# Four row tiles' neighbour lists, not two, made inside layer 1's loop of a four-layer graph network

## The chip, the cores and the metric

One core of a Trainium2 chip runs the whole kernel. The metric is the device time of one execution in microseconds, the median of three runs. The engines are TensorE (PE in the profile, its weight loads PEld), VectorE (DVE), ScalarE (ACT), GpSimd (POOL) and SyncE (SP), whose queue issues most transfers; ScalarE's queue issues the writes of the transposed matrix. Each engine and each queue works in order.

## The reference: what is computed

There are 2708 nodes with 128 features. The adjacency matrix `adj` (2708 x 2708, f32) is sparse, with values in [0.05, 1): some 16 entries a row, and the diagonal is always there. Each of four layers takes h = relu(layernorm(x)) and adds its result to x:

```python
# layer 0: mean over a node's columns
msg = jnp.matmul(H.T, X); inv_deg = 1.0 / H.sum(axis=0)
return msg * inv_deg[:, None]
# layer 1: a message for each pair (i, j), weighted by adj
s = node_feats @ msg_w[:, :D].T
d = node_feats @ msg_w[:, D:].T
messages = jax.nn.gelu(s[:, None, :] + d[None, :, :] + msg_b, approximate=False)
aggregated = jnp.einsum('ijd,ij->id', messages, adj)
new_feats = jnp.concatenate([node_feats, aggregated], -1) @ upd_w.T + upd_b
h = gelu(new_feats) + node_feats, then a layer norm with ln_w, ln_b
# layer 2: agg = adj @ states, then a GRU cell
# layer 3: graph attention with two heads, masked by adj > 0 or the diagonal
```

Only layer 1 needs to know which entries are not zero: a Gelu for each of 7.3 million pairs would be too much, so the kernel lists the entries.

## The kernel before, in words

**Tiles and lists.** Nodes come in 22 row tiles of 128 (the last has 20). Columns come in 22 blocks of 124. For each row tile n and block b, VectorE's `max` finds the eight largest values of each row and `max_index` their columns: one *list* (lines 357 and 359, in `list_cut`). A block that holds part of the diagonal is listed from a copy `near` with the diagonal blanked; a row tile has two such blocks.

**Layer 0's loop** (lines 541 to 586) goes over six column cuts c of 512 columns, and within each over six row groups s of four row tiles. Cuts 0 to 4 are steps of their own; the sixth (148 columns, tiles `z`) is worked beside the fifth. At each step VectorE lists the step's blocks (four per row tile), SyncE's queue issues the load of a later step into one of `RING` = 4 buffers (`rows_a`), and TensorE transposes the step's blocks and sums h times the matrix (`work_cut`): a *turn* is four transposes and one sum. ScalarE copies each transposed bank out into one of ten buffers (`turned`) and adds up the degrees on the way; the write of that buffer to `adjT` in device memory is issued one turn later. A load buffer is free when TensorE, VectorE and GpSimd have all read it.

Some lists are not made in this loop: for row tiles from `LATER` = 19 on (but the last, tile 21), the blocks away from the diagonal, 20 in each of tiles 19 and 20, are loaded again in layer 1's loop and listed there, `AT_ONCE` = 3 in a period (`load_late`, `list_late`). The last row tile, of 20 rows, is loaded in one piece at period `WIDE_AT` and listed by `list_wide`; `place_wide` moves these lists to their place by DMA.

**Between the layers** (lines 604 to 636 and 1082 to 1094) VectorE lists the sixth cut's blocks of tiles 4 to 21, and the first three row tiles are prepared for layer 1.

**Layer 1's loop** (`period`, line 1003) has one period for each row tile t and six blocks k in a period. In a period TensorE adds sources and destinations for tile t's entries in `combine` (six bf16 products for each block of 128 entries), ScalarE takes the Gelu (`activate`), and `gather` multiplies by the put tiles, which hold the adjacency values at their rows. Meanwhile the next three tiles go through a pipeline, all in program order on each engine:

- for tile t+4, `count_rows` counts the entries of each row and block;
- for tile t+3, `rank` (TensorE) sums the counts, `spread_ends`, `describe_next` and `select_rows` (all on VectorE, with ScalarE and GpSimd) split the f32 values in three bf16 parts and build the row selector `sel`; two DMAs shift it by one row, and `finish_rows` subtracts;
- for tile t+2, `fetch` (TensorE) brings the entries to their slots and `place` (VectorE) picks value and column;
- for tile t+1, `pass_on` sends the columns to all partitions by DMA, `columns` makes the equality tile `cols`; GpSimd (`put_values`) and ScalarE (`put_more`) make the put tiles.

Every second period `sources` prepares the source rows of the next two tiles. `split` cuts a value in three: ScalarE copies the lead part, VectorE subtracts it, ScalarE copies the second part, GpSimd subtracts.

**Updates.** After four row tiles (a group g; the groups are 0 to `LAST` = 5) the aggregate goes through `mix` (TensorE) and eight `update` steps: bias (VectorE), Gelu (ScalarE), residual and statistics (VectorE), factors (VectorE), scaling (ScalarE, then GpSimd), residual and statistics (VectorE), factors (VectorE), scaling to h (ScalarE). A table says at which period and block each step is issued. The last group's steps are issued in layer 2's first chunk (line 1464), between the pieces of `aggregate`, whose products read h and the transposed matrix.

The order of the instructions is the one in which the program issues them; no scheduler moves them.

## Time and profile before

| what | us |
|---|---|
| median of three runs (1030.32, 1031.84, 1036.13) | 1031.84 |
| the profiled execution | 1032.76 |
| its span, first to last instruction | 1031.0 |
| layer 0's loop, start of the span to its last sums | 0 to about 209 |
| between the layers | 209 to 262 |
| layer 1's periods, steady | 262 to 588 |
| layers 2 and 3 | 588 to 1031 |

TensorE is busy 922.2 us of the span, VectorE 797.4, ScalarE 532.7, GpSimd 470.9; the mean granted TensorE clock is 0.946. Of the line groups, 342 lists from load buffers take 78.9 us in `max` and 91.8 us in `max_index`.

How to read it: a row of a timeline is start, duration, engine, line, operation, output and inputs, shape, number of instructions, and in brackets the time that the engine sat idle before it and who released it. A row of the waits is engine, tile and line, then who was waited for: microseconds in total, how many times, the longest. The granted clock is a share of full speed. A matmul in f32 shows as two instructions. Busy times of PE contain the pipeline's overlap, so 26.00 of 26.00 says that there was no gap, not that the array was at its peak.

### The profile page before, as it was taken

The numbers are of one execution on the slowest core, as the hardware profiler recorded it, in microseconds if no ns is written. First come the engines' busy times: TensorE is split into PE (matmuls) and PEld (weight loads), VectorE is DVE, ScalarE is ACT, GpSimd is POOL, SyncE is SP. The second block draws the span as 40 slices with busy tenths as digits, with TensorE's granted clock in tenths as the row PEclk, the third lists the DMA queues.
The fourth block names the chain that finished last, engine by engine and source line by source line (L and its number), as shares of the span: only waits on it lengthen the run. The fifth ranks groups of instructions, "written<-read, shape, count | busy, mean of one in ns | idle before, by whom it ended". The sixth has DMA issues, their size and how long they took to land. (4 is left out here: it accounts for less than half of the span.)

```text
span 1031.0 us, 22163 instructions
## 1 busy us (share of the span) xinstructions
PE 922.2 (89%) x7948; PEld 747.7 (73%) x7948; DVE 797.4 (77%) x2753; ACT 532.7 (52%) x1561; POOL 470.9 (46%) x588
## 2 busy tenths in 40 slices
PE   6699798955899999999998899999888999999983
PEld 3355354624799999999998844444578999989972
DVE  7999798977677788977767366666578977997793
ACT  5755556734666666676675513333322543654342
POOL 6322222422977798897877264334311300340042
PEclk9999899955899999999999999999989999999996
DMA  9799799512333333333131455565311475457000
GB/s 298 260 314 374 248 365 389 209 65 84 102 121 110 119 109 114 124 101 115 66 114 56 156 187 188 187 204 201 111 48 46 143 233 182 135 164 240 5 15 16
DMA packets 83194, 162.90 MB, mean 158 GB/s; under 512 B 14672, under 2 KB 30148, under 8 KB 83074
## 3 DMA queue, kind: packets, MB, share of 16 engines
q1 hardware_dynamic: 63094, 129.25, 38.7%
q10 hardware_dynamic: 19980, 32.14, 8.6%
q8 instruction: 64, 1.05, 0.4%
q14 instruction: 56, 0.46, 0.1%
HBM read 114.74 MB, written 30.87 MB: 141 GB/s over the span
## 5 line engine op out<-in xcount | busy, mean ns | idle before, releaser
L806 POOL TENSOR_SCALAR put<-count,line,value 128x128 f32<-128x128 f32 x176 | 197.6, 1136 | 32.8 <-DVE value L795 32.6
L1187 PE MATMUL att<-hv,wt 128*128 128x129 f32 x1672 | 195.6, 278 | 7.8 <-DVE wt L1157 6.4
L1187 PEld LDWEIGHTS att<-hv,wt 128*128 128x128 f32 x1672 | 191.9, 194 | 10.9 <-DVE wt L1157 8.9
L888 PE MATMUL p_m<-s,sel 128*128 128x128 bf16 x1452 | 163.5, 221 | 8.5 <-ACT g L900 6.1
L892 PE MATMUL p_m<-d,cols 124*128 124x128 bf16 (+1 forms) x1452 | 163.5, 221 | 5.2 <-DVE cols L837 5.2
L1157 DVE SCALAR_TENSOR_TENSOR wt<-row,lift,mask 128x1024 f32<-128x1024 f32 (+1 forms) x132 | 138.8, 1082 | 22.1 <-PE att L1187 22.0
L120 POOL TENSOR_TENSOR n_r<-n_r,minus_half 128x4 f32<-128x4 f32 (+1 forms) x28 | 39.8, 1420 | 232.0 <-DVE n_r L119 226.9
L913 PE MATMUL agg<-put,g 128*128 128x128 f32 (+1 forms) x968 | 124.1, 281 | 0.0
L381 PE MATMUL sums<-a,h 128*128 128x512 f32 x220 | 119.4, 640 | 1.6 <-ACT h L136 1.6
L395 PEld LDWEIGHTS p_T<-ident,a 128*128 128x128 f32 (+1 forms) x440 | 55.4, 146 | 84.8 <-ACT aT L400 39.7
L913 PEld LDWEIGHTS agg<-put,g 128*128 128x128 f32 x968 | 114.7, 194 | 0.0
L888 PEld LDWEIGHTS <-sel 128*128 128x128 bf16 x1452 | 104.8, 98 | 10.6 <-issue 9.9
L1348 PE MATMUL p_agg<-a,hs 128*128 128x512 f32 (+2 forms) x264 | 108.4, 552 | 2.2 <-DMA a<-adjT 2.1
L892 PEld LDWEIGHTS <-cols 124*128 124x128 bf16 (+1 forms) x1452 | 103.8, 98 | 6.3 <-DVE cols L837 6.3
L395 PE MATMUL p_T<-ident,a 128*128 128x128 f32 (+1 forms) x440 | 73.3, 287 | 30.6 <-ACT aT L400 24.0
L815 ACT ACTIVATE put<-mine,value 128x128 f32<-128x128 bf16 x308 | 100.5, 391 | 0.0
L900 ACT ACTIVATE g<-p_m 128x512 f32<-128x512 f32 x132 | 72.7, 551 | 52.0 <-PE agg L913 41.0
L359 DVE FIND_INDEX8 col<-val,a 128x8 uint16<-128x124 f32 x342 | 91.8, 280 | 0.0
L357 DVE MAX8 val<-a 128x8 f32<-128x124 f32 x342 | 78.9, 271 | 7.6 <-DMA a<-in_adj 7.6
L1348 PEld LDWEIGHTS p_agg<-a,hs 128*128 128x128 f32 (+1 forms) x264 | 47.4, 192 | 49.8 <-issue 46.3
L400 ACT ACTIVATE aT<-p_T 128x512 f32<-128x512 f32 (+2 forms) x132 | 70.9, 539 | 23.9 <-PE p_T L395 18.4
L1310 ACT ACTIVATE hs<-hs 128x1354 f32<-128x1354 f32 (+1 forms) x44 | 58.5, 1329 | 39.3 <-DMA hs<-in_adj 38.9
(287 smaller groups left out, 1556.6 us busy)
## 6 DMA issues: line engine op xcount, KB each, us to landing
hs<-in_adj SPq DMA_DIRECT2D x42, 677.0 KB
adjT<-aT ACTq DMA_DIRECT2D x105, 256.0 KB
a<-adjT SPq DMA_DIRECT2D x20, 1280.0 KB
spread<-passed SPq DMA_DIRECT2D x22, 704.0 KB
later<-sel SPq DMA_DIRECT2D x22, 616.0 KB
a<-in_adj SPq DMA_DIRECT2D x5, 1152.0 KB
a<-in_adj SPq DMA_DIRECT2D x5, 1120.0 KB
a<-in_adj SPq DMA_DIRECT2D x5, 1088.0 KB
```

The lines of the kernel that those rows point to most:

```text
L357: nc.vector.max(val[0:m, n, b, :], v)
L359: nc.vector.max_index(col[0:m, n, b, :], val[0:m, n, b, :], v)
L381: nc.tensor.matmul(accs[c][:, 0:w], h0[0:m, n, :], a[0:m, n - g0, t0 * P - lo : t0 * P - lo + w], start=(n == 0), stop=(n == NT - 1),)
L395: nc.tensor.transpose(p[0:k, i * iw + q * P : i * iw + q * P + m], a[0:m, q, e : e + k], ident[0:m, 0:m])
L806: nc.gpsimd.tensor_scalar(st["put", 0][:, b, :], count, st["line"][:, b : b + 1], st["value"][:, b : b + 1], ALU.is_equal, ALU.mult,)
L815: nc.scalar.activation(st["put", 1][:, b - HP, :], st["mine"][:, b - HP, :], AF.Identity, scale=st["value"][:, b : b + 1])
L888: nc.tensor.matmul(p[:, b - b0, :], st["sel"][:, b, :], s3[:, q, t % 2, :], start=(q == 0), stop=False)
L892: nc.tensor.matmul(p[:, b - b0, :], st["cols"][0:kb, b, :], d3[0:kb, b, q, :], start=False, stop=(q == 2))
L913: nc.tensor.matmul(agg, g[:, b - 4 * k, :], put, start=(b == 0), stop=False)
L1157: nc.vector.scalar_tensor_tensor(wt[:, 0:n], row[:, k, c : c + n], lift[:, j, k : k + 1], mask[:, j, c : c + n], op0=ALU.max, op1=ALU.mult,)
L1187: nc.tensor.matmul(banks[s // 3][:, s % 3, :], wt[:, q * P : (q + 1) * P], hv[:, j, k, :], start=(v < 2 and s // 3 not in touched), stop=( ...
L1348: nc.tensor.matmul(pa[:, 0:n], h[0:k, j, :], a[0:k, j - j0, 0:n], start=(j == 0), stop=(j == NT - 1))
```

## The change

- `LATER` is NT - 5 = 17: lists of row tiles 17 to 20 away from the diagonal, 80 instead of 40, are made in layer 1's loop, `AT_ONCE` = 5 in a period: two at k = 1 and three at the period's end. `WIDE_AT` becomes 17 (it was 15).
- Layer 0 has five load buffers, and six write buffers for the transposed tiles.
- In a period, the describing of the next tile is cut in two. ScalarE's lead copy is issued at k = 1, the subtractions after `select_rows` at k = 2. `sources` is cut in the same way.
- The update steps are issued after `place`, `finish_rows` and the late loads of their block, two blocks later than before for most groups. The last two groups of layer 1's loop have tables of their own, and the final two steps of group 4 are issued in layer 2, after the last group's first two.
- `count_rows` of the last two tiles moves to the end of the period before.

```diff
--- before.py
+++ after.py
@@ -186,8 +186,9 @@
     for q in range(2):
         nc.gpsimd.tensor_copy(xb[q][:, :, 4 * S : 4 * S + R], part.unsqueeze(1).to_broadcast([P, NB, R]))
 
-    LATER = NT - 3
-    AT_ONCE = 3
+    LATER = NT - 5
+    AT_ONCE = 5
+    EARLY = 2
     WIDE = 4
 
     def near_blocks(n):
@@ -281,7 +282,7 @@
             scale_rows([dst[:, t + q, 0:D]], [xs[:, t + q, :]], r[:, q : q + 1], b[:, q : q + 1], AF.Relu)
             yield
 
-    RING = 4
+    RING = 5
     WINDOW = CH + 16 * (len(GROUPS) - 2)
     l0, ending = ExitStack(), ExitStack()
     ordered = ExitStack()
@@ -290,7 +291,7 @@
     once0 = l0.enter_context(tc.tile_pool(name="l0h", bufs=1))
     pool = l0.enter_context(tc.tile_pool(name="l0k", bufs=2))
     marked = l0.enter_context(tc.tile_pool(name="l0n", bufs=8))
-    turned = l0.enter_context(tc.tile_pool(name="l0t", bufs=10))
+    turned = l0.enter_context(tc.tile_pool(name="l0t", bufs=6))
     sump = l0.enter_context(tc.tile_pool(name="l0p", bufs=3, space=PSUM))
     turnp = l0.enter_context(tc.tile_pool(name="l0q", bufs=3, space=PSUM))
     h0 = once0.tile([P, NT, D], F32, name="h0")
@@ -611,11 +612,25 @@
         nc.scalar.copy(dst[1], rest)
         nc.gpsimd.tensor_tensor(dst[2], rest, dst[1], ALU.subtract)
 
-    def describe(t, rest):
+    def lead_of(dst, src):
+        nc.scalar.copy(dst[0], src)
+
+    def rest_of(dst, src, rest):
+        nc.vector.tensor_tensor(rest, src, dst[0], ALU.subtract)
+        nc.scalar.copy(dst[1], rest)
+        nc.gpsimd.tensor_tensor(dst[2], rest, dst[1], ALU.subtract)
+
+    def values_of(t):
+        return [xb[t % 2][:, :, q * S : (q + 1) * S] for q in range(3)], val[:, t, :, :]
+
+    def describe_columns(t):
         x = xb[t % 2]
-        split([x[:, :, q * S : (q + 1) * S] for q in range(3)], val[:, t, :, :], rest)
         nc.gpsimd.tensor_copy(x[:, :, 3 * S : 4 * S], col[:, t, :, :])
         nc.gpsimd.tensor_copy(x[:, :, C - 1], ends[:, t, :])
+
+    def describe(t, rest):
+        split(*values_of(t), rest)
+        describe_columns(t)
 
     for n in range(4, 14):
         list_last(n)
@@ -689,15 +704,15 @@
             units = late_blocks[(t - 1) * AT_ONCE : t * AT_ONCE] if t > 0 else []
             if not units:
                 return
-            cols = work.tile([P, WIDE, JB], F32, name="cols_a")
+            cols = work.tile([P, AT_ONCE, JB], F32, name="cols_a")
             state["late", t] = []
             for i, (n, b) in enumerate(units):
                 m, k = size(n), width(b)
                 nc.sync.dma_start(cols[0:m, i, 0:k], adj[n * P : n * P + m, b * JB : b * JB + k])
                 state["late", t].append((n, b, cols[0:m, i, 0:k]))
 
-        def list_late(t):
-            units = state.pop(("late", t), [])
+        def list_late(t, first, last):
+            units = state.get(("late", t), [])[first:last]
             for n, b, a in units:
                 nc.vector.max(val[0 : size(n), n, b, :], a)
             for n, b, a in units:
@@ -707,7 +722,7 @@
         pieces = [(b, min(WIDE, NB - 1 - b)) for b in range(0, NB - 1, WIDE)]
 
         def load_wide():
-            cols = state["wide"] = work.tile([P, WIDE, JB], F32, name="cols_a")
+            cols = state["wide"] = work.tile([P, AT_ONCE, JB], F32, name="cols_a")
             for i, (b, k) in enumerate(pieces):
                 nc.sync.dma_start(
                     cols[i * TAIL : (i + 1) * TAIL, 0:k, :],
@@ -735,6 +750,10 @@
 
         def describe_next(t):
             describe(t, once.tile([P, NB, S], F32, name="v_r"))
+
+        def describe_rest(t):
+            rest_of(*values_of(t), once.tile([P, NB, S], F32, name="v_r"))
+            describe_columns(t)
 
         def select_rows(t):
 
@@ -866,8 +885,14 @@
                     mq = size(2 * k + q)
                     nc.vector.tensor_tensor(sb[0:mq, q, :, :], pv[0:mq, q, :, :], bv[0:mq, :, :], ALU.add)
             s3 = three.tile([P, 3, 2, D], BF16, name="s3")
-            rest = once.tile([P, 2, D], F32, name="s_r")
-            split([s3[:, q, :, :] for q in range(3)], sb[:, :, 0, :], rest)
+            lead_of([s3[:, q, :, :] for q in range(3)], sb[:, :, 0, :])
+            state["sb"] = sb
+            own_rows[k] = s3, None
+
+        def sources_rest(k):
+
+            sb, s3 = state.pop("sb"), own_rows[k][0]
+            rest_of([s3[:, q, :, :] for q in range(3)], sb[:, :, 0, :], once.tile([P, 2, D], F32, name="s_r"))
             gs = three.tile([P, 2, D], F32, name="gs")
             nc.scalar.activation(gs, sb[:, :, 1, :], AF.Gelu)
             for q in range(2):
@@ -981,14 +1006,14 @@
         GB = (NB + 3) // 4
         mixes, updates = {}, {}
         for g, (first, n) in enumerate(GROUPS[:-1]):
-            at, apart = (first + n + 1) * GB + 1, GB
-            if g == LAST - 2:
-                apart = GB // 2
-            elif g == LAST - 1:
-                at, apart = at - GB + 2, 1
-            mixes[divmod(at, GB)] = g
-            for step in range(STEPS):
-                updates.setdefault(divmod(at + 1 + step * apart, GB), []).append((g, step))
+            at = (first + n + 1) * GB
+            mixes[divmod(at + 1 if g < LAST - 1 else at - 3, GB)] = g
+            steps = {
+                LAST - 1: [at - 2, at - 1, at, at + 1, at + 2, at + 5],
+                LAST - 2: [at + 4, at + GB + 4, at + 2 * GB + 4, *(at + 3 * GB + q for q in (0, 1, 2, 4, 5))],
+            }.get(g, [at + 4 + step * GB for step in range(STEPS)])
+            for step, when in enumerate(steps):
+                updates.setdefault(divmod(when, GB), []).append((g, step))
 
         def check_lists():
             over = fix.tile([P, 2], F32, name="over1")
@@ -1035,23 +1060,28 @@
                 if k in (1, 2) and b:
                     fetch(t + 2, k - 1)
                 if k == 1 and a:
-                    describe_next(t + 3)
+                    lead_of(*values_of(t + 3))
+                if k == 1:
+                    list_late(t, 0, EARLY)
+                    if t == WIDE_AT:
+                        list_wide()
                 if k == 2:
                     if now and t % 2 == 0 and t + 2 < NT:
                         sources(t // 2 + 1)
                     if a:
                         select_rows(t + 3)
-                    if now and t + 4 < NT:
+                        describe_rest(t + 3)
+                    if now and t % 2 == 0 and t + 2 < NT:
+                        sources_rest(t // 2 + 1)
+                    if now and t + 4 < NT - 2:
                         count_rows(t + 4)
-                for g, step in updates.pop((t, k), ()):
-                    update(g, step)
                 if k == 1 and t == NT - 2:
                     check_lists()
                 if k > 0 and c:
                     put_more(t + 1, k)
                 if k == 3 and c:
                     columns(t + 1)
-                if k == 3 and t == WIDE_AT + 1:
+                if k == 3 and t == WIDE_AT:
                     place_wide()
                 if k == 3 and b:
                     place(t + 2)
@@ -1061,10 +1091,12 @@
                     load_late(t + 1)
                     if t + 1 == WIDE_AT:
                         load_wide()
+                for g, step in updates.pop((t, k), ()):
+                    update(g, step)
                 if k == GB - 1:
-                    list_late(t)
-                    if t == WIDE_AT:
-                        list_wide()
+                    list_late(t, EARLY, AT_ONCE)
+                    if now and NT - 2 <= t + 4 < NT:
+                        count_rows(t + 4)
 
 
         def fetch_both(t):
@@ -1084,7 +1116,7 @@
             (finish_rows, 0), (fetch_both, 0), (spread_ends, 1), (select_rows, 1), (rows, 4),
             (split_destinations, 3), (turn_rows, 4), (place, 0), (destinations, 4), (pass_on, 0), (list_last, 18),
             (finish_rows, 1), (fetch_both, 1), (split_destinations, 4), (destinations, 5), (spread_ends, 2),
-            (select_rows, 2), (sources, 0), (describe_next, 2), (columns, 0), (place, 1), (split_destinations, 5),
+            (select_rows, 2), (sources, 0), (sources_rest, 0), (describe_next, 2), (columns, 0), (place, 1), (split_destinations, 5),
             *((list_last, n) for n in range(19, NT)),
             (close_lists, 0),
         ):
@@ -1465,11 +1497,14 @@
             pa = accs.tile([P, CH], F32, tag=f"acc{g % 2}", name="p_agg")
             if g == 0:
                 update(LAST, 0)
+                update(LAST, 1)
+                update(LAST - 1, 6)
+                update(LAST - 1, 7)
             for i, j0 in enumerate(range(0, NT, PIECE)):
                 aggregate(t0, k0, pa, j0)
                 if g > 0:
                     continue
-                for step in ((1, 2), (3, 4), (5,), (6, 7), ())[i]:
+                for step in ((2,), (3, 4), (5,), (6, 7), ())[i]:
                     update(LAST, step)
                 if i == 2:
                     nc.gpsimd.memset(mask[:, NT - 1, :], 0)
```

## The prediction

> **What bounds the kernel now.** I read the page's slices first, then busy times by stretch, then the chain of waits on each side of the places the change touches, last the instruction lists there. Three stretches matter: layer 0's loop (up to 209 us), layer 1's loop (262 to 588) and the first sums of layer 2 (588 to 614). Columns: stretch, its length, busy time of TensorE (PE), its weight loads, VectorE (DVE), ScalarE (ACT), GpSimd (POOL), granted clock, DMA share, GB/s.
>
> ```profile
> 26.00:52.00 26.00, 17.77 (x66) 9.10 (x64) 26.00 (x176) 18.30 (x70) 9.21 (x33) 0.93 0.77 261
> 52.00:78.00 26.00, 26.00 (x118) 15.03 (x119) 25.90 (x177) 15.43 (x59) 4.94 (x12) 1.00 0.96 315
> 78.00:104.00 26.00, 24.75 (x118) 14.64 (x117) 25.39 (x171) 15.23 (x56) 6.92 (x24) 1.00 1.03 373
> 104.00:130.00 26.00, 20.43 (x69) 9.94 (x68) 19.02 (x124) 14.89 (x61) 7.25 (x16) 0.84 0.79 251
> 130.00:156.00 26.00, 25.45 (x123) 15.38 (x122) 25.75 (x170) 13.57 (x46) 6.50 (x20) 0.96 1.03 365
> 156.00:182.00 26.00, 21.28 (x108) 13.00 (x107) 21.79 (x148) 15.57 (x58) 4.60 (x11) 1.00 1.05 389
> 182.00:208.00 26.00, 23.64 (x138) 16.36 (x136) 25.86 (x166) 21.51 (x77) 12.61 (x36) 1.00 0.52 194
> 208.00:262.00 54.00, 26.39 (x153) 17.70 (x151) 39.21 (x143) 21.32 (x71) 14.87 (x25) 0.52 0.20 67
> 262.00:588.00 326.00, 315.96 (x4468) 310.16 (x4468) 245.60 (x602) 211.37 (x639) 261.80 (x260) 0.98 0.34 111
> 588.00:614.00 26.00, 23.24 (x54) 10.12 (x54) 14.09 (x40) 4.11 (x12) 16.01 (x16) 0.87 0.37 117
> ```
>
> In layer 0 VectorE has no room in five of the seven stretches, and its two gaps (104 to 130, 156 to 182) are waits for loads. TensorE is close behind, DMA at or above a share of 1 in three. In layer 1 TensorE is the bound (316.0 of 326), VectorE at 75%. What a layer-0 load waits for, how fast lists go, and the load that came late:
>
> ```profile
> SPq L317 <- PE sums L381: 40.7, 13, 6.3
> SPq L317 <- DVE col L359: 39.1, 9, 8.6
> ...
> SPq L323 <- DVE col L359: 12.5, 3, 5.5
> ```
>
> ```profile
> 81.46 0.46 DVE L357 MAX8 val<-a 128x8 f32<-128x124 f32 x2
> ...
> 82.35 0.46 DVE L357 MAX8 val<-a 128x8 f32<-128x124 f32 x2
> ...
> 130.15 0.48 DVE L357 MAX8 val<-a 128x8 f32<-128x124 f32 x2 [6.26 <-DMA a<-in_adj]
> ```
>
> Two lists take 0.89 us, so a list costs **0.446 us**. A load waits for a buffer that VectorE or TensorE still holds. At 130 a buffer was not filled in time: the clock went to half.
>
> In layer 1 and behind it, TensorE's own waits:
>
> ```profile
> 446.01 0.33 PE L888 MATMUL p_m<-s,sel 128*128 128x128 bf16 x3 [1.57 <-ACT g L900]
> 506.62 0.33 PE L888 MATMUL p_m<-s,sel 128*128 128x128 bf16 x3 [1.84 <-ACT g L900]
> 543.51 0.34 PE L892 MATMUL p_m<-d,cols 124*128 124x128 bf16 x3 [2.25 <-DVE cols L837]
> 591.09 0.79 PE L944 MATMUL p_u<-upd_wT,aggT 128*128 128x128 f32 x2 [2.76 <-ACT aggT L927]
> ```
>
> ```profile
> DVE v_r L610 <- ACT xb L609: 36.0, 16, 3.9
> ...
> DVE s_r L610 <- ACT s L609: 12.6, 10, 1.3
> ```
>
> The last fence is VectorE idle 48.6 us of layer 1 in front of the two subtractions, waiting for a ScalarE copy that stands behind other ScalarE work.
>
> **The change, part by part.** The profiled execution took 1032.76 us (span 1031.0, 1.8 around it); the median of the three runs is 1031.84. I sum against 1032.76.
>
> 1. *Lists out of layer 0.* Row tiles 17 and 18 have 22 blocks each, two of them near the diagonal and kept: 40 lists go (423 to 383). Of these 32 stand in the first four column sweeps, 4 in the fifth, 4 after the loop. The loop's 36 are 36 x 0.446 = 16.1 us of VectorE. The 4 late ones (1.8 us) sit beside waits for the shifted rows and I cost them at nothing; at most 0.9 us of them is exposed, before the second tile's shift.
> What is late next? Floors from 26 to 182 (156 us): VectorE is busy 143.9, less 32 x 0.446 = 14.3, so 129.6. TensorE is busy 135.7, less 7.0 lost to half clock (26 x 0.07, 0.16 and 0.04), so 128.7. DMA moved 58.6 MB from 0 to 182 (26 us times each row's GB/s, with 299 for 0 to 26), and at the best row's 389 GB/s needs 151 of those 182. All three would allow more than 16.1, but they now stand within a few per cent of each other and take turns. Bounds: 0 (another bound takes all) and 23.7 (16.1 plus the 7.6 that VectorE waited for loads). I take **-14**: VectorE's busy stretches are what the trace shows as full, and a little is lost to turn-taking.
> A rule speaks against this. The Trainium skill, "DMA: Bandwidth & Descriptors", section Specifications, puts the HBM limit of a core at about 358 GB/s. The trace has a stretch at 389 and one at 373, so it does not hold as a ceiling here; by it DMA would need 164 of 182 us, an estimate, and the gain would still not be cut below 14.
>
> 2. *Five load buffers, six write buffers.* A load is issued one step earlier, which covers the 6.26 above and helps reach the 14. The transposed tiles' buffers fall from ten to six. In the trace's landing events a write lands 2 us after its issue when nothing loads and 6 to 8 us when loads run. A turn of TensorE is 1.30 us (four transposes and a sum). A copy must find the write of six turns before landed: six turns are 7.8 us; copy, one turn of delay and a write of 6.7 us are 0.6 + 1.3 + 6.7 = 8.6. So it could cost 0.8 us in six turns, 18 times in 110 turns: 15 us at worst for 6.7, nothing where latency is only queueing (five writes in flight at 1.30 us each are the 6.7, and fewer in flight land sooner). Bounds 0 and +15; I take 0, because ScalarE never waits for its copy's buffer now and latency and number in flight agree.
>
> 3. *The end of layer 0.* TensorE waits 3.10 us at 212 for the copy that closes VectorE's lists. With VectorE no longer behind, bounds 0 and -3.1: **-2**.
>
> 4. *Lists into layer 1.* 40 x 0.446 = 17.8 us of VectorE, five lists a period in 16 periods where three stood in 14. VectorE goes from 245.6 to 263.4 of 326. Two of the five stand where VectorE waited for ScalarE (the 36.0). ScalarE's lead copy of the next tile's values now runs while VectorE lists and builds the row selector, and the subtraction comes behind. The same for the sources (12.6). Update steps stand behind the placing, no longer ahead of it, so the equality tiles (the 2.25), the row numbers and TensorE's fetch are no longer behind up to 5.4 us of statistics (537.0 to 542.4 in the list). TensorE's idle time is 10.0 us of 326 and half clock costs 0.02 x 326 = 6.5, part of it the start. Bounds: -14 (nearly all of that goes) and +17.8 (all lists on TensorE's path). I take **-6**: the waits named belong to the order that is changed, and VectorE keeps 60 us free.
> ScalarE has a new wait, for the subtraction that now follows the 1.6 us selector. Queued behind it are the second source copy, the Gelu of the own row and put tiles, then g, for which TensorE waits. It gains the slot before. GpSimd's queue keeps its order; its third part of the values comes one block later, for a fetch a period off. On SyncE's queue two more loads of 62 KB a period stand behind the shift of the selector, 0.45 us of issue each: free, at a DMA share of 0.34.
> The page just named (same section) says pieces under 512 B run below line rate; the new loads' rows are 496 B. Its only price here is DMA time in a layer with two thirds of it idle: 0 by both.
>
> 5. *The last list-group's update.* Its final two steps (factors, scaling) move behind the last group's first two. ScalarE's scaling of 1.65 us waited 3.40 for VectorE, and the copy of the aggregate stood behind it: TensorE's 2.76 us at 591. Half clock there costs 26 x 0.13 = 3.4 us. But the last tiles' rows are needed 20 products later (17 us at 0.86), where they now land with about 1 us to spare, so part comes back. Bounds 0 and -6.2; **-4**.
>
> Sum: -14 - 2 - 6 - 4 = -26: 1032.76 - 26 = 1006.8, against the median 1005.8. I say 1006.
>
> **The rivals.**
> - *Layer 0 is bound by TensorE and DMA all along* and gives half. For: TensorE 26.00 of 26.00 from 52 to 78, DMA share over 1 in three rows. Against: both floors are 27 to 31 us below the stretch. -7 there, -1, -4, -3 elsewhere: 1018.
> - *Layer 1 takes it back*: VectorE, late by lists, becomes the bound there. For: VectorE was already busy 14.4 of 15 us in one stretch (413 to 428) and TensorE lost time in it. Against: the waits it is freed of are more than the lists. Gains -16 in layer 0 and -4 after, all 17.8 on the path: 1032.76 - 20 + 17.8 = 1031, no change.
> - *Six write buffers throttle ScalarE* (the other side). For: 8.6 against 7.8 us. With latency L a group of six turns costs L + 1.9 - 7.8 more, 18.3 times. The whole gain of 26 and 5 us more is gone at L = 7.6; at 8.0 it is 38 lost: 1006 + 38 = 1044. So it decides when writes, with one more load in flight, take over 7.6 us in the mean rather than their 6.7. Against: fewer writes in flight land sooner.
> - *The change does not do what it says*: no; the five lists and the order are in the built program, and 383 and 80 lists can be counted.
>
> **How the numbers follow.** About 0.5% (5 us) is what can be told from no change. Forecast case 0.62 (992 to 1013); half gain 0.21 (1013 to 1025); layer 1 takes it back 0.08; write buffers 0.09. Faster: 0.62 + 0.21 = 0.83; same 0.08; slower 0.09. The range is 992 to 1025: low, layer 0 at 23.7 and layer 1 at -10; high, the half-gain rival with some of the write buffers' price.
>
> **What would show it.** Right: layer 0's last sums end near 194 instead of 208; no VectorE wait near 6 us for a load in the loop; layer 1 at 80 lists, VectorE waits before the subtraction of values down from 36 to under 12, TensorE's idle under 6 us in layer 1; no wait at the aggregate's copy. Wrong: ScalarE waiting for write landings in layer 0; a TensorE period over 15.1 us with VectorE named; lists of the last tiles late, so that the ranking product waits for counts at the loop's end.

## The result, and the profile after

The changed kernel takes **1024.76 us** (median of five runs, 1020.77 to 1026.56) against 1031.56 (1030.32 to 1036.13): a ratio of 0.9922, 95% interval 0.9894 to 0.995. It is 0.8% faster, by 7 us and not by the predicted 26. The profiled execution took 1026.56 us, its span is 1024.8.

Four marks cut both spans into the prediction's steps. They are starts of TensorE's products: the last sum of the sixth cut (the 208 of the prediction), the first and the last `combine` product of layer 1, and the first product with `W_msgT` in layer 2.

| stretch, us | before | after | moved | predicted |
|---|---|---|---|---|
| to the sixth cut's last sum | 208.3 | 211.0 | +2.7 | -14 |
| from there to the first `combine` | 39.5 | 39.3 | -0.2 | -2 |
| first to last `combine` | 336.5 | 329.9 | -6.6 | -6 |
| last `combine` to the first `W_msgT` product | 31.6 | 27.6 | -4.0 | -4 |
| the rest | 415.1 | 417.0 | +1.9 | 0 |
| span | 1031.0 | 1024.8 | -6.2 | -26 |

Layer 1 and the step behind it came out as predicted in size. Nearly all of the error (17 of 20 us) lies in layer 0: 40 lists left it and it did not become shorter. Busy times by stretch of the changed kernel (columns as in the prediction):

```profile
52.00:78.00 26.00, 26.00 (x118) 15.00 (x117) 25.90 (x174) 15.62 (x59) 5.43 (x14) 1.00 0.94 318
78.00:104.00 26.00, 24.42 (x87) 12.89 (x86) 21.35 (x144) 13.46 (x50) 6.81 (x24) 0.80 0.94 313
104.00:130.00 26.00, 21.69 (x94) 12.05 (x93) 18.45 (x121) 14.80 (x58) 6.64 (x14) 0.93 0.83 260
...
156.00:182.00 26.00, 22.19 (x93) 12.11 (x92) 11.44 (x77) 17.36 (x68) 5.31 (x13) 0.93 1.04 378
...
262.00:588.00 326.00, 316.82 (x4479) 310.22 (x4479) 263.16 (x732) 214.43 (x653) 256.98 (x263) 0.98 0.38 119
588.00:614.00 26.00, 25.82 (x66) 11.56 (x66) 16.22 (x42) 6.92 (x14) 16.36 (x15) 1.00 0.64 214
```

VectorE, nearly full in layer 0 before, is now idle for more than half of 156 to 182 (11.44 of 26), and TensorE is hardly fuller (22.19, before 21.28). Behind layer 1 TensorE has next to no gap and full clock (25.82 of 26 at 1.00; before 23.24 at 0.87). Where VectorE's time went, in its waits from 26 to 210 us, first before and then after:

```profile
DVE val L357 <- DMA a<-in_adj: 7.6, 3, 6.3
DVE inv_deg L430 <- ACT aT L400: 4.1, 1, 4.1
```

```profile
DVE inv_deg L431 <- ACT aT L401: 26.1, 3, 14.5
DVE val L358 <- DMA a<-in_adj: 2.4, 3, 1.4
```

The wait for late loads is gone, as foreseen. In its place VectorE stands 26.1 us in `invert`, which needs the degree sums that ScalarE makes while it copies the transposed tiles out. VectorE now runs ahead of everybody and waits for the same ScalarE that TensorE waits for. That last part could be read before. These are TensorE's gaps of 1 us and more from 26 us to the end of layer 0's loop in the kernel *before*:

```profile
28.16 0.66 PE L395 MATMUL p_T<-ident,a 128*128 128x128 f32 x4 [1.78 <-ACT aT L400]
35.33 0.66 PE L395 MATMUL p_T<-ident,a 128*128 128x128 f32 x4 [1.77 <-ACT aT L400]
...
46.07 0.66 PE L395 MATMUL p_T<-ident,a 128*128 128x128 f32 x4 [2.67 <-ACT aT L400]
82.00 0.66 PE L395 MATMUL p_T<-ident,a 128*128 128x128 f32 x4 [1.25 <-ACT aT L400]
109.81 0.66 PE L395 MATMUL p_T<-ident,a 128*128 128x128 f32 x4 [1.20 <-ACT aT L400]
120.47 0.92 PE L395 MATMUL p_T<-ident,a 128*128 128x128 f32 x4 [3.82 <-ACT aT L400]
...
158.88 0.66 PE L395 MATMUL p_T<-ident,a 128*128 128x128 f32 x4 [1.78 <-ACT aT L400]
171.03 0.66 PE L395 MATMUL p_T<-ident,a 128*128 128x128 f32 x4 [2.94 <-ACT aT L400]
184.64 0.66 PE L395 MATMUL p_T<-ident,a 128*128 128x128 f32 x4 [1.98 <-ACT aT L400]
```

Every one names ScalarE's copy and none names VectorE. ScalarE was busy only 13.6 to 18.3 of 26 us in the stretches from 26 to 182. Why an engine with so much room is late shows in the changed kernel, here ScalarE's list around 80 us (ACTq is ScalarE's queue issuing a transfer), and then TensorE's:

```profile
78.33 0.59 ACT L401 ACTIVATE aT<-p_T 128x512 f32<-128x512 f32 x1
78.80 0.20 ACT L401 ACTIVATION_READ_ACCUMULATOR aT<-p_T 128x1 f32 x1
82.60 0.38 ACTq L366 DMA_DIRECT2D adjT<-aT  x1
83.03 0.40 ACT L264 ACTIVATE junk<-xs,flat 128x128 f32<-128x128 f32 x1 [4.02 <-DMA a<-in_adj]
...
83.43 0.57 ACT L401 ACTIVATE aT<-p_T 128x512 f32<-128x512 f32 x1
```

```profile
81.59 1.02 PE L382 MATMUL sums<-a,h 128*128 128x512 f32 x2
84.15 2.17 PE L396 MATMUL p_T<-ident,a 128*128 128x128 f32 x8 [1.54 <-ACT aT L401]
86.25 4.08 PE L382 MATMUL sums<-a,h 128*128 128x512 f32 x4
```

ScalarE stood 4.02 us in front of the *issue* of a write, and what ended it was the landing of a load that has nothing to do with that write. In the trace's landing events the transfers issued by SyncE and ScalarE take turns at eight semaphores (101 to 108). The load issued at 72.26 had semaphore 104 and landed at 82.53; the write that is next on 104 was issued at 82.60, 76 ns later, with only two other transfers in flight. TensorE then ran out of banks for 1.54 us, and four sum instructions, of which two take 1.02 us at full clock, took 4.08: the half clock of the row 78 to 104. The kernel before shows the same ahead of TensorE's longest gap, the 3.82 us that end at 120.47:

```profile
114.89 0.19 ACT L400 ACTIVATION_READ_ACCUMULATOR aT<-p_T 128x1 f32 x1
118.98 0.33 ACTq L365 DMA_DIRECT2D adjT<-aT  x1
119.35 0.40 ACT L263 ACTIVATE junk<-xs,flat 128x128 f32<-128x128 f32 x1 [4.27 <-DMA W_hhT<-in_W_hhT]
...
119.75 0.58 ACT L400 ACTIVATE aT<-p_T 128x512 f32<-128x512 f32 x1
```

It is no single case: of the 86 writes that ScalarE issued between 26 and 182 us there, 23 left within 150 ns of the landing of the transfer before them on their semaphore, and 19 of these 23 transfers were loads. In its waits between 26 and 210 us ScalarE stood 32.5 us, 12 times, for landings in the kernel before, each time with the issue of a write right ahead of the instruction that was late. After, it stood 27.0 us, 13 times: 18.3 us of them (8 times) with such an issue ahead, the rest in front of its copies, where 4.8 us (4 times) are waits for one of the six write buffers.

The time to the mark hides two opposite movements. From 26 us to the mark TensorE sat idle 22.7 us before and 19.2 after, and was busy 159.7 us before and 165.9 after, with the same number of instructions, at a mean clock of 0.96 and 0.93. So the change did take 3.5 us from TensorE's waits, and the longer stay at half clock (some 14 us before, some 27 after) took more than that back.

### The profile page after: what moved, and what is told of

Read it like the earlier page. It is cut to its first block, busy times and chain, and to the rows that moved or that the text cites. A ratio compares the mean times of both kernels' runs of the same rounds, so it can differ in the third digit from the quotient of the medians.

```text
span 1024.8 us, 22209 instructions
## 1 busy us (share of the span) xinstructions
PE 925.0 (90%) x7948; PEld 748.9 (73%) x7948; DVE 796.3 (78%) x2753; ACT 533.6 (52%) x1561; POOL 460.2 (45%) x588
## 5 line engine op out<-in xcount | busy, mean ns | idle before, releaser
L825 POOL TENSOR_SCALAR put<-count,line,value 128x128 f32<-128x128 f32 x176 | 195.1, 1120 | 11.7 <-PE agg L938 10.6
L120 POOL TENSOR_TENSOR n_r<-n_r,minus_half 128x4 f32<-128x4 f32 (+1 forms) x28 | 39.5, 1412 | 243.4 <-DVE n_r L119 238.2
L382 PE MATMUL sums<-a,h 128*128 128x512 f32 x220 | 124.4, 664 | 1.6 <-ACT h L136 1.6
L401 ACT ACTIVATE aT<-p_T 128x512 f32<-128x512 f32 (+2 forms) x132 | 71.0, 539 | 37.4 <-PE p_T L396 27.9
L360 DVE FIND_INDEX8 col<-val,a 128x8 uint16<-128x124 f32 x306 | 82.3, 281 | 0.0
L358 DVE MAX8 val<-a 128x8 f32<-128x124 f32 x306 | 70.8, 272 | 2.4 <-DMA a<-in_adj 2.4
```

The lines of the kernel that those rows point to most:

```text
L360: nc.vector.max_index(col[0:m, n, b, :], val[0:m, n, b, :], v)
L382: nc.tensor.matmul(accs[c][:, 0:w], h0[0:m, n, :], a[0:m, n - g0, t0 * P - lo : t0 * P - lo + w], start=(n == 0), stop=(n == NT - 1),)
L825: nc.gpsimd.tensor_scalar(st["put", 0][:, b, :], count, st["line"][:, b : b + 1], st["value"][:, b : b + 1], ALU.is_equal, ALU.mult,)
```

## The experiments

The theory after this comparison, **S**: layer 0 is set by TensorE with ScalarE's copies, and ScalarE stands in issues of writes; VectorE's lists are beside that. The rivals: the six write buffers took the gain (**B**), the new wait in `invert` took it (**W**), or the lists were paid back elsewhere (**V**). All kernels at a glance; the marks are those of the first table. Each ratio is to the kernel before as measured beside that kernel (medians from 1029.85 to 1032.79 us), so kernels are better compared by ratios than by medians. The marks come from one profiled execution each, which can lie some us off its kernel's median: 1026.56 us for the changed kernel, 1023.06 for *lists twice* (median 1028.91).

| kernel | median us | ratio to before, 95% | sixth cut's last sum | first `combine` | `combine` | behind |
|---|---|---|---|---|---|---|
| before | 1031.56 | | 208.3 | 247.8 | 336.5 | 31.6 |
| after | 1024.76 | 0.9922 (0.9894 to 0.995) | 211.0 | 250.3 | 329.9 | 27.6 |
| order alone | 1025.45 | 0.9934 (0.991 to 0.9959) | 210.0 | 249.5 | 329.3 | 29.3 |
| old buffers | 1022.80 | 0.9891 (0.9857 to 0.9926) | 208.9 | 246.2 | 329.9 | 29.3 |
| inverse later | 1020.89 | 0.9888 (0.9831 to 0.9944) | 212.4 | 247.9 | 329.1 | 28.0 |
| lists twice | 1028.91 | 0.9961 (0.9937 to 0.9985) | 209.5 | 249.8 | 329.0 | 27.9 |
| weights later | 1018.91 | 0.9878 (0.9838 to 0.9917) | 208.1 | 243.6 | 329.5 | 27.7 |
| writes by GpSimd | 1014.09 | 0.9833 (0.9798 to 0.9868) | 198.9 | 237.1 | 329.7 | 29.3 |
| paired writes | 1017.05 | 0.9869 (0.9842 to 0.9896) | 199.9 | 240.6 | 329.8 | 27.9 |
| half writes | (1018.12, one run) | | 200.1 | 241.7 | 331.8 | 28.0 |
| all four edits, GpSimd | 1008.97 | 0.9774 (0.9738 to 0.9809) | 193.4 | 231.6 | 329.5 | 29.3 |
| the same, lists twice | 1015.20 | 0.984 (0.9793 to 0.9888) | 199.0 | 237.5 | 329.8 | 29.3 |
| the same, paired writes | 1008.74 | 0.9759 (0.9722 to 0.9796) | 190.9 | 231.6 | 332.0 | 29.3 |
| before, writes by GpSimd | 1023.45 | 0.9907 (0.9871 to 0.9943) | 198.9 | 238.3 | 334.7 | 31.7 |
| writes by SyncE | 1022.90 | 0.992 (0.9896 to 0.9944) | 205.8 | 247.4 | 331.2 | 29.2 |
| all four edits, SyncE | 1005.61 | 0.9745 (0.9719 to 0.9771) | 188.4 | 227.0 | 330.3 | 29.3 |
| writes by SyncE, old buffers | 1010.45 | 0.9807 (0.9791 to 0.9823) | 195.0 | 233.5 | 330.8 | 27.9 |
| before, writes by SyncE | 1017.97 | 0.9881 (0.9865 to 0.9898) | 195.9 | 236.6 | 334.5 | 31.3 |

**Order alone** (the changed kernel without its moved lists and buffers; this edit and those below are shortened):

```diff
-    LATER = NT - 5
-    AT_ONCE = 5
+    LATER = NT - 3
+    AT_ONCE = 3
-    RING = 5
+    RING = 4
-    turned = ... name="l0t", bufs=6
+    turned = ... name="l0t", bufs=10
```

> The changed kernel with its lists put back: two row tiles (40 lists) in layer 1, three a period, four load buffers, ten write buffers; the order of the period, the cut describing and the update tables stay. Theory S (layer 0's loop is held by TensorE and by ScalarE and loads waiting for transfers, so that lists moved out of it bought nothing): last sums of layer 0 near 208 us as before, layer 1 (first to last of its combine products) near 329 us or 1 to 3 below, 4 us saved behind it: 1020 to 1023 us, as fast as the changed kernel (1025) or faster. Rival V (the 40 lists did shorten something in layer 0 that was then lost): the same layer 0, but the lists cost layer 1 at least 6 of their 17.8 us, so that layer 1 falls to 323 or less here: 1015 us or less.

Measured: 1025.45 us, the changed kernel's time but 2.5 above S's range, with layer 1 at 329.3 as S expected, and V falls: 40 lists cost layer 1 at most 0.6 us (329.3 without, 329.9 with). **Nearly the whole measured gain is the new order.** What the lists bought layer 0 is read against *old buffers*, which differs from this kernel by the lists alone: the mark moved from 210.0 to 208.9, TensorE's idle time before it from 22.4 to 20.1 us, the median by 2.7 us with intervals that overlap. That is 0 to 3 us, and not 14. VectorE's waits in layer 1, first of this kernel and then of the changed one (before: 36.0 and 12.6):

```profile
DVE v_r L619 <- ACT xb L616: 8.3, 5, 3.7
...
DVE s_r L619 <- ACT s L616: 3.0, 9, 1.0
```

```profile
DVE ends L1042 <- PE p_r L536: 12.2, 9, 2.0
DVE sb L882 <- PE p_s L865: 7.7, 7, 1.5
...
DVE v_r L619 <- ACT xb L616: 3.9, 4, 1.3
...
DVE s_r L619 <- ACT s L616: 3.2, 9, 1.0
```

VectorE's two largest waits now name TensorE, the bound of layer 1, which is where waiting is free.

**Old buffers, inverse later, lists twice.** Three edits of the changed kernel, one each:

```diff
-    RING = 5
+    RING = 4
-    turned = ... name="l0t", bufs=6
+    turned = ... name="l0t", bufs=10
```

> The changed kernel with four load buffers and ten write buffers, as before; the lists stay out of layer 0. Theory S: last sums within 3 us of the changed kernel's 210.5, time 1022 to 1027. Rival B (VectorE's lists set the loop and six write buffers took the gain): last sums at 194 to 198, time 1010 to 1014, and ScalarE's waits for landings fall by over 8 us.

```diff
-                if c > 0 and s == (1 if c < LAST - 1 else 0) and n == g0 + 2:
+                if c > 0 and s == (2 if c < LAST - 1 else 1) and n == g0 + 1:
                     invert(c - 1)
```

> The changed kernel with the inverse of the degrees, where VectorE stood 26.1 us for ScalarE's sums, issued one step later, just ahead of its reader. Rival W (this wait is what took the gain): it shrinks below 5 us, last sums of layer 0 at 194 to 200, time 1010 to 1016. Theory S: it shrinks too, VectorE waits for loads in its place, last sums within 3 us of 210.5, time 1022 to 1027.

```diff
-            elif n < LATER:
+            elif n < NT - 3:
                 units.insert(0, (b, cuts[c, s][...]))
```

> The changed kernel with the 40 lists of row tiles 17 and 18 made in layer 0 as well (and again in layer 1): 36 x 0.446 = 16 us of VectorE's work put back in the loop. Theory S: the waits of VectorE in the loop (26.1 at the inverse) take it, last sums within 3 us of 210.5, time 1022 to 1028. Rivals B and W (VectorE is on the path in the loop, its gain eaten elsewhere): last sums later by 8 to 16 us, time 1033 to 1041.

Measured: last sums at 208.9, 212.4 and 209.5, all within 3 us of 211.0, so neither B's 194 to 198, nor W's 194 to 200, nor 8 to 16 us for lists put back. The time of the second is 1020.9, below S's range of 1022, with a wide spread (1016 to 1027); its wait in `invert` fell to 8.8 us, not below 5, and its waits for loads rose to 14.0. The third's median is 1028.9, 0.9 above S's range, so up to 4 of its 16 us may be real, all the more as its mark is from one of its fastest executions. In that execution the wait in `invert` fell from 26.1 to 14.2 us: the lists were made in time that VectorE otherwise waited. VectorE was not the bound.

**What does hold layer 0.** Four kernels change transfers and leave VectorE alone.

```diff
-        if (c, s) == (2, 3):
+        if (c, s) == (LAST - 1, 3):
             W_msgT, W_ihT, W_hhT = load(late, "W_msgT"), ...
```

> The changed kernel with the loads of the later layers' weights issued at the loop's last cut, row group 3 (about 180 us), and no longer at cut 2, row group 3, where they meet the loop's loads and writes between 104 and 130 us. Theory S (transfers in flight hold layer 0): DMA work taken out of a full stretch does what VectorE work taken out did not do: TensorE's busy time in 104 to 130 rises from 21.7 to over 24 of 26, last sums of layer 0 at 203 to 207 instead of 211, time 1017 to 1021. Rival C (the loop follows TensorE's clock and its copies by ScalarE, transfers are beside it): last sums within 2 us of 211, time 1023 to 1027.

```diff
-            nc.scalar.dma_start(*written.pop())
+            nc.gpsimd.dma_start(*written.pop())
```

> The changed kernel with the writes of the transposed tiles issued by GpSimd instead of ScalarE; bytes and number of transfers are the same. Theory S1 (an issue that has to wait for an earlier transfer blocks ScalarE, and with it the copies TensorE waits for): ScalarE's waits for landings (27 us in the loop) fall below 8, last sums of layer 0 at 198 to 205, time 1012 to 1020. Rival S2 (bandwidth: the bytes set the loop, whoever issues them): last sums within 3 us of 211, time 1022 to 1028. If GpSimd is blocked in its turn, its normalisation chain for cut 0 and its masks come late, which shows as ScalarE and VectorE waiting for GpSimd.

```diff
+            two = gk == 4 == tk
+            second = two and (js[0] - t0) % 2 == 1
+            if not second:
+                pair = turned.tile([P, 2 * CH], F32, name="aT")
+            aT = pair[:, CH : 2 * CH] if second else pair[:, 0:CH]
...
+            if second:
+                written.append((
+                    adjT[0:k, js[0] - 1 : js[0] + 1, i0 : i0 + iw], pair[0:k, :].rearrange("p (j i) -> p j i", j=2)
+                ))
```

> The changed kernel with four load buffers, and with one write for two turns in the first five cuts where a group has four row tiles: 512 KB each, half as many issues, five buffers of double size. To be compared with four load buffers and ten single write buffers (1022.8). Theory S1: fewer issues on ScalarE that can block, its waits for landings in the loop fall by a third or more, last sums 3 to 8 us earlier than 208.9, time 1015 to 1020. Rival S2: same bytes, last sums within 3 us of 208.9, time 1021 to 1025.

```diff
-                adjT[0:k, js[0] : js[0] + n, i0 : i0 + iw], aT[0:k, 0 : n * iw]...
+                adjT[0:min(k, 64), js[0] : js[0] + n, i0 : i0 + iw], aT[0:min(k, 64), 0 : n * iw]...
```

> The changed kernel, but each write in layer 0 carries only half of its partitions (64 of 128, 15 MB less in the loop, the same number of issues); the other half of the transposed matrix is filled with wrong numbers by one transfer a period in layer 1, so that layers 2 and 3 compute with a wrong matrix. Only layer 0 is read. Theory S2 (bytes): the loop moves a quarter less, last sums of layer 0 at 190 to 202 instead of 211. Theory S1 also gains, since smaller writes land sooner, but at least 4 us. Rival C (neither: TensorE, its clock and ScalarE's copies): last sums within 3 us of 211.

Measured: taking the weights' loads out of 104 to 130 filled that stretch (TensorE 25.07 of 26 at full clock, against 21.69 at 0.93) and gave 4 to 6 us (by the ratios and by the medians), the last sums 3 us earlier where 4 to 8 were expected. Writes by GpSimd, paired and halved ended the sums 12, 9 and 11 us earlier: all three act on the writes, none on lists, and C (transfers are beside it) falls. S2, that bytes set the loop whoever issues them, falls with GpSimd and with pairs, which move the same bytes. With pairs ScalarE's waits for landings fell from 33.3 us (old buffers) to 23.3, a little less than the third expected. S1's account was off in one thing: with GpSimd issuing, ScalarE's waits for landings were to fall below 8 us and were 23.7. They are no longer waits in an issue but for a write buffer. With ten buffers that wait is gone too, as the next group shows.

**Does it hold for the kernel before, and what are the lists worth when ScalarE is free?** "All four edits" is writes by GpSimd, old buffers, inverse later and weights later.

> The changed kernel with all that helped layer 0 so far: writes issued by GpSimd, four load buffers and ten write buffers, the inverse of the degrees one step later, the weights' loads at the last cut. Theory S1 (the loop was held by blocked issues on ScalarE): the 23.7 us that ScalarE waited for six write buffers go, last sums of layer 0 at 186 to 196 (writes by GpSimd alone: 198.9), time 1002 to 1011. Rival S2 (with the issues free, bytes or TensorE are the bound at once): last sums at 196 to 200, time 1010 to 1015.

> The kernel with all four edits, and the 40 lists of row tiles 17 and 18 made in layer 0 as well: 16 us of VectorE's work in the loop. If lists count once ScalarE is free (VectorE stood just behind it): last sums 6 to 16 us later than without, time up by 6 to 16 us. If VectorE is off the path here too: last sums within 3 us, time within 4 us.

> The kernel before with one edit: writes of the transposed tiles issued by GpSimd; its lists stay in layer 0, its buffers are ten and four. Theory S1 (the kernel before was held by ScalarE's blocked issues too, not by its lists): last sums of layer 0 at 196 to 202 instead of 208.3, time 1019 to 1025. If VectorE's lists held it, as predicted: last sums within 3 us of 208, time 1028 to 1034.

> The kernel with all four edits and one write for two turns (512 KB), five buffers of double size. If GpSimd's work of issuing (17 of 26 us busy with single writes, 6 without) or the number of transfers still costs: last sums 2 to 6 us earlier than with single writes, time 2 to 6 us less. If not: within 2 us, or later by 1 to 3 us since a buffer is held longer.

Measured: all four edits 1008.97 us, sums at 193.4, ScalarE's waits for landings 0.8 us. The kernel before, its 40 lists in place, gains 0.9% (some 10 us) by the one edit (sums 198.9). And now the lists count: put back beside the four edits, they end the sums 5.6 us later (199.0 against 193.4) and cost 6.2 us, at the low end of the 6 to 16 expected. VectorE is idle only 0.6 of the 173 us before the mark there. So the prediction's mechanism exists, but only behind the one that it missed. Pairs on top bring nothing in time (1008.74), though their mark is 2.5 us earlier.

**ScalarE's standing, or the eight semaphores?** GpSimd's writes had semaphores of their own, so that run changed two things. Writes on SyncE's queue keep the eight and free ScalarE; the edits are `nc.sync.dma_start` for `nc.scalar.dma_start`, without and with the others.

> The changed kernel with the writes of the transposed tiles issued on SyncE's queue, between the loads; ScalarE issues none. In the trace of the changed kernel the transfers of SyncE's and ScalarE's queues share eight landing semaphores (101 to 108), and GpSimd's writes had others, so moving writes to GpSimd changed two things. Theory S1a (ScalarE standing in an issue is what cost): last sums of layer 0 at 196 to 204 as with GpSimd (198.9), time 1012 to 1019. Rival S1b (eight semaphores for loads and writes together limit what is in flight, whoever issues): SyncE stands in their place, loads come late, last sums at 207 to 215, time 1021 to 1029.

> The kernel with all four edits, its writes issued on SyncE's queue instead of GpSimd's. Theory S1a: last sums within 3 us of 193.4, time 1005 to 1012 (GpSimd, which computes descriptors for 17 of 26 us, is relieved). Rival S1b: last sums 199 or later, time 1015 or more, VectorE and TensorE waiting for loads.

> The changed kernel with writes on SyncE's queue, and four load and ten write buffers. With six write buffers ScalarE waited 35.3 us for them and the last sums of layer 0 ended at 205.8. If six write buffers are what then held the loop: that wait falls below 15 us, last sums at 192 to 199, time 1008 to 1015. If the eight shared semaphores held it (they stay): last sums within 3 us of 206, time 1019 to 1026.

> The kernel before with one edit, its writes on SyncE's queue; ten write buffers, lists in layer 0. If ScalarE's blocked issues held the kernel before: last sums of layer 0 at 192 to 202 instead of 208.3, time 1015 to 1025, as with GpSimd (198.9, 1023.5). If VectorE's lists held it: last sums within 3 us of 208, time 1028 to 1034.

Measured: the first landed between the two theories (205.8; 1022.9). The reason is one line each in the waits of ScalarE, first with five load and six write buffers, then with four and ten:

```profile
ACT aT L401 <- DMA adjT<-aT: 35.3, 16, 7.2
```

```profile
ACT aT L401 <- DMA adjT<-aT: 18.1, 7, 4.7
```

With ten the sums end at 195.0 and the time is 1010.45: ten write and four load buffers in place of six and five are worth some 12 us (1022.90 to 1010.45, 11.7 by the ratios) once ScalarE issues nothing. The expected fall of the wait below 15 us came out at 18.1. With all four edits SyncE is the best issuer: its mark is 188.4, 5 us earlier than GpSimd's where within 3 was expected, and its time **1005.61 us**, 0.9745 of before and the fastest kernel here. So sharing the eight semaphores is not itself what cost most: in that kernel 38 of 74 transfers between 26 and 104 us were issued within 150 ns of the landing before them on their semaphore, and SyncE stood there instead of ScalarE. VectorE waited 7.3 us for loads in this loop, in 3 waits, and TensorE for none. TensorE's remaining gaps of 1 us and more in its layer-0 loop from 26 us on:

```profile
28.32 0.65 PE L396 MATMUL p_T<-ident,a 128*128 128x128 f32 x4 [1.78 <-ACT aT L401]
35.49 0.66 PE L396 MATMUL p_T<-ident,a 128*128 128x128 f32 x4 [1.78 <-ACT aT L401]
42.66 0.66 PE L396 MATMUL p_T<-ident,a 128*128 128x128 f32 x4 [1.77 <-ACT aT L401]
...
140.56 0.66 PE L396 MATMUL p_T<-ident,a 128*128 128x128 f32 x4 [1.20 <-ACT aT L401]
164.59 0.66 PE L396 MATMUL p_T<-ident,a 128*128 128x128 f32 x4 [1.94 <-ACT aT L401]
170.39 0.66 PE L396 MATMUL p_T<-ident,z 128*128 128x128 f32 x4 [1.10 <-ACT aT L401]
```

The last run is the plainest: the kernel *before* with its writes on SyncE, one word changed, takes 1017.97 us. By the ratios (0.9881 and 0.9922) that is some 4 us less than the changed kernel, with intervals that just overlap. Of the 12.5 us by which its mark is earlier than the kernel before's, 6.8 are idle time of TensorE (22.7 to 15.9) and 5.7 busy time (159.7 to 154.0, at a mean clock of 0.99 for 0.96). Its sums end at 195.9 with 40 lists in layer 0, those of the changed kernel with the same queue and buffers at 195.0 without them: 16 us of VectorE's work for 0.9 us.

## Why the prediction was wrong, point by point

1. *Lists out of layer 0, -14: wrong, the step that failed.* The prediction put it that "VectorE's busy stretches are what the trace shows as full". They were full because VectorE had work and ran ahead, not because TensorE waited for it: 14 us were forecast for 36 lists, and what the lists alone bought is 0 to 3 us. The floors were compared (129.6, 128.7, 151 of 182), but the list of TensorE's gaps, each naming `aT`, was read in layer 1 and not in layer 0. Two readings went wrong on the way. Of VectorE's two gaps that were put down to loads, the second was its wait in `invert` for ScalarE (4.1 us, until 166.01). And the half clock that was put down to the buffer not filled at 130 had begun at 121.9 (0.50 from there to 132.2, 1.00 from 104 until there), after TensorE's gap of 3.82 us, which names ScalarE's copy. What held ScalarE were its own issues; that lists did not hold the loop is shown by three pairs of kernels (last sums with and without the lists in layer 0: 210.0 and 208.9, 209.5 and 211.0, 195.9 and 195.0); with all four edits they count (199.0 and 193.4).
2. *Five load and six write buffers, 0: right in size, wrong in reason.* Undone alone it is 1022.80 against 1024.76, inside the spread. The prediction said that ScalarE never waits for its copy's buffer. That was true of ten buffers, where it stood in issues before it could get to that wait. With six it waits 4.8 us in the changed kernel, and 23.7 to 35.3 us once it issues nothing.
3. *The end of layer 0, -2: wrong, nothing came.* TensorE's wait for the copy closing the lists is 3.50 us (before 3.10). VectorE stood 14.46 us in the last `invert` until 170.87 (before 4.11 until 166.01), so the lists that this copy stands behind were begun 5 us later, not earlier; from 182 to 208 VectorE is full in both (25.86 of 26).
4. *Lists into layer 1 and the new order, -6: right in size, -6.6, and partly in mechanism.* TensorE's idle time from first to last `combine` (336.9 and 330.3 us) fell from 18.3 to 15.5 us, its busy time from 318.6 to 314.8, at a clock of 0.98 for 0.96. So 2.8 us are fewer waits and 3.8 are busy time at a higher clock; which edit raised the clock no run separates. VectorE is busy 267.1 us for 252.5. The price of the lists was at most 0.6 us, so the order earned all of it. The sign "waits before the subtraction under 12 us" came true (3.9); "TensorE's idle under 6 us" did not: 9.2 us of the 326 from 262 to 588, 10.0 before.
5. *The last list-group's update, -4: right, -4.0, with some luck in the size.* TensorE's 2.76 us for the aggregate's copy is gone and the clock there is 1.00. But of the fifteen kernels with the new order seven show 27.6 to 28.0 us in this stretch and eight 29.2 or 29.3, 2.3 less than before, though the edits between them lie elsewhere.

Of the rivals, *layer 0 is bound by TensorE and DMA all along* holds the result in its range (1013 to 1025, at the edge), but it put 7 us of gain in layer 0 where there was none, and DMA counted by way of ScalarE's issues. *Six write buffers throttle ScalarE* named a real limit that was not yet the binding one: its condition, writes of over 7.6 us in the mean, did not come (5.4 us from issue to landing between 26 and 182 us in the changed kernel). *Layer 1 takes it back*, whose 1031 is about as near to the result, is refuted by layer 1's 329.9 us. The sign "ScalarE waiting for write landings in layer 0" stood there under *wrong*, and something close to it was already to be seen before: 32.5 us in 12 waits for landings, ten of them a load's.

What stays open: why some gaps of TensorE start ten microseconds of half clock (1.54 us at 84) and others do not (1.8 us at 28 and 35, with the clock at 1.00 until 47), how much of the differences in layer 0 is this clock's own, and how much of the 6.6 us between the old-buffer kernel on SyncE and the one with all four edits (195.0 to 188.4) belongs to the inverse and how much to the weights.

## What to carry to other kernels

A full engine is a candidate for the bound and no more: list the gaps of the engine that ends last, see whom each one names, and ask of that engine why it was late, above all when it was busy for only 60% of the time. Count the issue of a transfer as an instruction that may wait, and keep large transfers off the queue of an engine whose next instruction somebody needs; when such a wait is taken away, look at once at the buffers behind it. A change in several parts is worth the sum only of the parts that lie on the path: run each part alone before the whole is believed.

## What the runs showed of the hardware that was not expected

- An issue on ScalarE's queue waits for the landing of a load issued by SyncE, if the two follow each other on one of the eight semaphores: 82.60 behind 82.53, with two other transfers in flight. The Trainium skill, "DMA: Bandwidth & Descriptors", section "Anatomy of one DMA — SWDGE (gpsimd) path", says that a semaphore wait of a DMA happens on the issuing sequencer before dispatch. The trace agrees for ScalarE's queue too: 4.02 us of ScalarE's time there.
- Who issues the same bytes moved layer 0 by 9 to 12 us (208.3 to 198.9 on GpSimd's queue, to 195.9 on SyncE's). With all four edits SyncE is 5 us ahead of GpSimd (188.4 to 193.4), which was busy 15 to 19 of 26 us while it issued the writes, 6 to 9 while it did not.
- With writes by GpSimd a stretch moved 402 GB/s (130 to 156 us), and in the loop an issue found up to 13 other transfers in flight instead of 7.
